# Sums of adj's quarters issued singly and after the first batch's split, with the planner's ranks set anew

## The chip, the core and the metric

The kernel runs on one core of a Trainium2 chip. The metric is the device time of one execution in microseconds (us). Five engines work side by side, each through its own instructions in a fixed order: TensorE (PE, matrix products and transposes), VectorE (DVE), ScalarE (ACT), GpSimd (POOL) and SyncE (SP, which here issues nearly all DMAs). They wait for each other by semaphores.

## The reference, cut to what matters

`x` is 16 batches of 1024 nodes with 128 features, `adj` one symmetric 1024 x 1024 matrix of zeros and ones. A graph attention layer comes first, then five steps of a gated recurrent unit over the graph, and each of the two is followed by a residual sum and a layernorm:

```python
h = x @ others_weight
e = leaky_relu(u1[:, idx1] + u2[:, idx2])           # u1 = h @ a1, u2 = h @ a2
att = softmax(where(adj > 0, e, NEG_BIG), axis=1)
x = layernorm(x + einsum('bik,bkl->bil', att, h) + x @ self_weight)

def step(h, _):
    m_in = einsum('nm,bmd->bnd', adj, h)             # m_out is the same product
    av = concatenate([m_in, m_out], axis=-1)
    u3 = h @ u3_w.T + u3_b
    z = sigmoid(av @ w3_w.T + w3_b + u3)
    r = sigmoid(av @ w4_w.T + w4_b + u3)
    hv = tanh(av @ w5_w.T + w5_b + (r * h @ u5_w.T + u5_b))
    h = (1.0 - z) * h + z * hv
# five steps, then
x = layernorm(x + h)
```

The product that costs most is `adj @ h`, done once for each batch and step.

## The kernel before, in words

**A planner sets the order.** The program doesn't emit its instructions where it describes them. Each piece of work is handed to `Plan.add` (L55) with its engine, an assumed length, a rank (smaller is more urgent), the function that emits it, and what it reads and writes. `Plan.order` (L74) then goes through a list schedule: whenever an engine is free in its assumed time, it takes the ready piece with the smallest rank. Only the resulting order is kept. It is emitted, and on the chip every engine works through it strictly as it stands, each piece held up by semaphores until what it reads is there. The assumed lengths and lags decide nothing else. The ranks come from `rank_of(b, s)` for a batch's step (ten more for each pair of batches, 4.2 more for each step), from `rank0(b)` for a batch's attention layer, and from a table of small offsets `D`: `m` for the copies of an adj product out of PSUM, `pu`, `pr`, `pz`, `pv` for the products of the gates, `u`, `r`, `z`, `hv` for their ScalarE work and `h` for VectorE's update of the state, `tr` and `o` for the way out of a step and of the kernel, `l1` to `l8` for the stages of the attention layer. `l3` is the stage in which the scaled features are split (below).

**Layer 0** (`layer0(b)`) computes, for each batch, the features `hx` with one 131-wide product per 128 nodes (L652), the exponentials of the logits, their sums over the neighbours (L807, DVE, with `adj` as a mask), and scales `rz` (L826 to L834). For batch 0 `rz` comes in two halves of four columns. Then each 128-row piece of `hx` is scaled and split into two fp32r numbers, a rounded upper half on ACT (L856) and the remainder, the lower half, on DVE (L862). Both halves for both of the two scalings lie in four `blk` tiles of four pieces. PE multiplies them by `adj` (`ps_acc_po`, L615), adds the residual (L919, L933), turns the result back (L565), and a layernorm follows (L521 and L523 on DVE, L527 to L534 on POOL, L542 on ACT). `own_weights` (L467) prepares the weights and biases of layer 1. `ahead` (L444) computes the residual products of batches 4 to 7 early (`ps_ahead`, L455) from loads of `x` into the tiles `r_x` and `z_x`; the planner gives these products to PE where nothing more urgent is ready.

**Layer 1** works on pairs of batches. For six of the forty pair-steps (`PLAIN`) `messages` uses plain products with the four quarters Y11, Y12, Y21, Y22 of `adj`: eight accumulating products for each half of a batch (`ps_acc`, L615). For the others it uses a scheme of seven products instead of eight, in which sums of quarters of `adj` (T1 to T4, the tile `tab`, 4 x 4 pieces of 128 x 512) are multiplied by sums of the pair's states (`s1` to `s4`). Its seven products share the banks a, b and c (`ps_acc_a`, `gz`, `ps_acc_c`), and in bank a the results are copied out while the accumulation goes on (L1130 to L1164). `gates` then computes for each half of a batch the gates r and z and the candidate hv: u (L1186) into a bank, copied to `gz` on ACT (L1189), products with `m` (L1196), tanh (L1199), r*h on DVE (L1206), products L1212 and L1213, tanh (L1221), and three DVE operations that update `hT` (L1224, L1227, L1230). `leave` turns `hT` and sends it through DRAM to the next step (T, X, G), or through PE (L565), split again by L603 and L607. Sixteen `look_at` pieces load halves of `adj` once more, one at a time through one buffer (`look`), and count zeros and ones on DVE (L1386, L1372).

**The lines that the change touches.** `sums_of_adj(c)` (L499) makes the four table pieces for row group c. Before, it is two pieces of planned work of two DVE operations each, which always stand together:

```python
dve(2 * V, 1 + c / 4, t13, reads=y, writes=[(("tab",), c, 0)])
dve(2 * V, 1 + c / 4, t24, reads=[*y, (("tab",), c, 0)], writes=[(("tab",), c, 1)])
```

Their rank is 1 to 1.75, larger than that of batch 0's attention (`first` is -62), so that the planner puts them where DVE would otherwise be idle; they can start once the four quarters are in SBUF.

Of the kernel before, what the change touches and what calls it, by code (L numbers as in the profile page):

```python
# [19 lines left out]
NC = N // P  # L20
# [117 lines left out]
def kernel(  # L138
# [79 lines left out]
    def exact(pools):  # L218

        def pool(name, bufs, space=None):  # L220
# [5 lines left out]
        tab = table.tile([P, 4, NC // 2, HALF], F32R, tag="tab", name="tab")  # L226
# [28 lines left out]
            "rstd": (3, [P, 2, 4], F32, None),  # L255
            "D": (6, [P, HALF], F32, bass.MemoryType.DRAM),
            "X": (24, [P, HALF + 16], F32, bass.MemoryType.DRAM),
# [30 lines left out]
        R, F, TR, V, A = 233, 858, 109, 605, 640  # L288
# [4 lines left out]
        def dve(*a, **k):  # L293
            plan.add("DVE", *a, **k)
# [5 lines left out]
            plan.add("SP", *a, **k)  # L300


        D = dict(m=-0.4, pu=1.4, u=1.2, pr=0.8, pz=1.4, r=1.7, pv=1.0, z=1.3, hv=-0.6, h=1.6, tr=1.6, o=5.8, ln=2.9)
        D.update(out=4.4, l1=-9, l2=-4, l3=-3, l4=-4, l5=-7, l6=-1.5, l7=-1, l8=-2)

        def on_pe(b, what):

# [6 lines left out]
        def rank_of(b, s):  # L314
            return 10 * (b // 2) + 4.2 * s + (LATER if b == B - 1 and plain(b // 2, s) else 0)

        def rank0(b):
            return 10 * (b // 2) - 1 * (1 - b % 2) + -1.0 - 6 * (b // 2 == 1)
# [21 lines left out]
        def early_loads():  # L340
# [28 lines left out]
            writes=[(boot, "early"), (ws, "early"), (x0, "early"), (("xt", 1), "early"), *((t, "early") for k in staged for t in k)],  # L369
# [97 lines left out]
        def own_weights():  # L467
            pb_ = ("ps", "g", "b")
            pe(150, -4.6, lambda: column_(pb_, slice(2 * P, 3 * P), 5), reads=[(ws, "b"), (("rz", 0), 1)], writes=[(pb_, 0)])
            dve(160, -4.3, lambda: nc.vector.tensor_copy(bias, T(pb_)[:, 0:5]), reads=[(pb_, 0)], writes=[(("bias",), 0)])  # L470
            dve(1000, -4.2, sums, reads=[(boot, "late"), (("bias",), 0), (("uw",), 0), (("rz", 0), 1)], writes=[(("wm",), 0)])

        def adj_tables(c):
            st = staged[c // 2]

            def left(copy):
                copy(adj[:, c, 0:HALF], T(st[0])[:, c % 2])

            def right():
                nc.scalar.activation(adj[:, c, HALF:N], T(st[1])[:, c % 2], AF.Identity, accum_out=cnt[:, c : c + 1])  # L480

            if c < 4:
                dve(420, -60, lambda: left(nc.vector.tensor_copy), reads=[(st[0], 0)], writes=[(("A",), c, 0)])
            else:
                act(A, -60, lambda: left(nc.scalar.copy), reads=[(st[0], 0)], writes=[(("A",), c, 0)])
            act(640, -50, right, reads=[(st[1], 0)], writes=[(("A",), c, 1)])
# [12 lines left out]
        def sums_of_adj(c):  # L499
            def f(x):  # L500
                return x(c).bitcast(F32)

            def t13():
                nc.vector.tensor_tensor(T1(c), f(Y11), f(Y12), ALU.subtract)
                nc.vector.tensor_tensor(T3(c), f(Y22), f(Y12), ALU.subtract)

            def t24():
                nc.vector.scalar_tensor_tensor(T2(c), f(T1), -1.0, f(Y22), ALU.mult, ALU.subtract)
                nc.vector.scalar_tensor_tensor(T4(c), f(T2), -1.0, f(Y21), ALU.mult, ALU.subtract)

            y = [(("A",), c + 4 * i, j) for i in range(2) for j in range(2)]
            dve(2 * V, 1 + c / 4, t13, reads=y, writes=[(("tab",), c, 0)])
            dve(2 * V, 1 + c / 4, t24, reads=[*y, (("tab",), c, 0)], writes=[(("tab",), c, 1)])


        def layernorm(key, g, rank, after, src, dst, write, sg=1, short=False):
# [108 lines left out]
        def layer0(b):  # L625

            first = rank0(b) - (60 if b == 0 else 0)
            rank = first + D["l1"]
            xt, hx, pb, u, us, uu, ud = (
# [147 lines left out]

            rank = first + D["l2"]

# [19 lines left out]

            rank = rank0(b) + D["l2"]  # L800
            junk = ("junk", b)
# [42 lines left out]
            if b == 0:  # L844
                own_weights()
            rank = rank0(b) + D["l3"]
            size = 1 if b == 0 else 4
# [196 lines left out]
        def messages(q, s, k):  # L1044
# [8 lines left out]
            def from_dram(b, g, i):  # L1053
                t, x = ("G", b, s, g), ("X", b, s, g)
                turn = [(("turn",), k, i - 1) if i else (("turn",), k - 1, 3)]
                entered = [(("hT", x), "in") for x in (one, two)] if s == 0 else []
                sp(0, rank, lambda: T(t), reads=[(x, 0), *turn, *entered], writes=[(t, "place"), (("turn",), k, i)], lag=0)
                back(x, t, rank, [(t, "place")])
                return t
# [34 lines left out]
            if plain(q, s):  # L1094
                for b in (one, two):
# [5 lines left out]
                    for e in range(2):  # L1101
                        bank, m = ("ps", "acc", b, s, e), ("m", b, s, e)
                        for g in range(2):
# [5 lines left out]
                            reads=[(bank, 0)],  # L1109
                            writes=[(m, 0)],  # L1110
# [1 line left out]
                return [[(("m", b, s, e), 0) for e in range(2)] for b in (one, two)]  # L1112

            blk = {k: ("blk", q, s, k) for k in ("x11", "x12", "x22", "s1", "s2", "s3", "s4")}
            t = [(("tab",), c, k) for c in range(4) for k in range(2)]
            f11, f12, f21, f22 = (from_dram(x, g, 2 * (x == two) + g) for x in (one, two) for g in range(2))
            halves(blk["x11"], f11)
            halves(blk["x12"], f12)
# [10 lines left out]
            a, b, c = (("ps", "acc", q, s, "a"), ("gz", q, s), ("ps", "acc", q, s, "c"))  # L1129
            m = {(x, e): ("m", x, s, e) for x in (one, two) for e in range(2)}  # L1130
# [276 lines left out]
        ahead()  # L1407
        for c in range(NC):
            adj_tables(c)
        for c in range(NC // 2):  # L1410
            sums_of_adj(c)
        for b in range(B):
            layer0(b)
        pairs = [(q, s) for q in range(B // 2) for s in range(STEPS)]
        for k, (q, s) in enumerate(sorted(pairs, key=lambda x: rank_of(2 * x[0], x[1]))):
            soon = messages(q, s, k)
            for b in (2 * q, 2 * q + 1):
                gates(b, s, soon)
                leave(b, s)
        for i in range(2 * NC):  # L1420
# [6 lines left out]
            reads=[  # L1427
                *((("seen",), b, k) for b in range(B) for k in range(2)),
                *((("count",), i) for i in range(2 * NC)),
                (("bad",), 0),  # L1430
                (("bad",), 1),
            ],
            writes=[(("rstd", "ends"), 0)],
# [6 lines left out]
            reads=[(("ps", "t", "flag"), 0)],  # L1440
            writes=[(("flag",), 0)],
# [208 lines left out]
    with ExitStack() as pools:  # L1650
        exact(pools)
# [51 lines left out]
```

## Time and profile before

| what | value |
|---|---|
| time, median of 3 runs | 1466.1 us (1465.45 to 1467.84) |
| the profiled execution, its own time | 1464.59 us |
| its span | 1462.4 us (2.2 us lie around it) |
| granted TensorE clock, mean | 0.996 |
| PE busy | 1440.0 us, 98% of the span, 5026 instructions |
| DVE busy | 1163.3 us, 80%, 2752 instructions |
| ACT busy | 896.7 us, 61%, 1792 instructions |
| POOL busy | 205.2 us, 14%, 323 instructions |
| DMA | 174.20 MB, 119 GB/s over the span |
| one 512-wide table sum (L504, L505, L508, L509) | 0.68 to 0.69 us each, 16 of them, 22.2 to 85.1 us from the start |
| landing of a `look` load, where the profile could match it | 2.6 us |

A busy share is an average over stages. An engine at 98% leaves 2% of time in which it wasn't working, and where that time lies, and what ended each of those waits, is what tells of a change of order. The profile has for that the waits by engine, with what released each; the timeline, with the idle time ahead of an instruction in square brackets; and the windows, which give the busy time of each engine within a stretch of the span.

### The profile page before, as it was taken

To read this page: it belongs to the slowest core of one execution; us is meant where nothing else is said; L and a number is where in the kernel's file an instruction comes from. 1 tells how busy PE (TensorE), PEld (TensorE's weight loads), DVE (VectorE), ACT (ScalarE), POOL (GpSimd) and SP (SyncE) were. 2 spreads that over 40 slices of the span, in tenths; PEclk is the share of its full clock that TensorE was granted. 3 is DMA by queue.
4 is the path that set the end of the run, shared out by engine and by line. 5 is a ranking of instruction groups with operands and counts; after the bars stand their busy time and mean duration, and the time that the engine had idled before them with its cause. 6 is when DMAs were issued, how large, how long until landed. Compare 5 with 4: busy or idle time off the path is not lost.

```text
span 1462.4 us, 17792 instructions
## 1 busy us (share of the span) xinstructions
PE 1440.0 (98%) x5026; PEld 901.1 (62%) x5026; DVE 1163.3 (80%) x2752; ACT 896.7 (61%) x1792; POOL 205.2 (14%) x323
## 2 busy tenths in 40 slices
PE   8999999999999999999999999999999999999996
PEld 7666666656566666665666556666666665656663
DVE  6895788978888888888988788886999877766434
ACT  5566564666656665766655776566666656554543
POOL 0321000113110130110301121101201103000201
PEclk9999999999999999999999999999999999999998
DMA  7425234555344553454434543455433544223201
GB/s 251 137 73 180 73 87 134 148 163 154 84 137 127 158 135 97 137 145 138 109 108 130 162 134 88 118 148 167 125 86 93 159 140 109 70 70 87 72 0 31
DMA packets 188033, 174.20 MB, mean 119 GB/s; under 512 B 34240, under 2 KB 137367, under 8 KB 187927
## 3 DMA queue, kind: packets, MB, share of 16 engines
q1 hardware_dynamic: 182562, 156.41, 38.3%
q0 software_dynamic: 4800, 15.73, 3.3%
q8 instruction: 41, 0.67, 0.2%
q10 hardware_dynamic: 564, 0.85, 0.2%
q14 instruction: 66, 0.53, 0.1%
HBM read 95.68 MB, written 77.24 MB: 118 GB/s over the span
## 4 chain that ended last, share of the span: by engine, by line
PE 88%; DMA 4%; DVE 3%; ACT 1%; issue 1%; SPq 1%; POOL 1%; POOLq 0%; DVEq 0%; ACTq 0%
PE ps_acc_a L615 17%; PE ps_g_r L1186 9%; PE ps_g_r L1196 9%; PE ps_g_v L1213 8%; PE gz L1196 8%; PE ps_g_v L1212 8%; PE ps_acc_c L615 8%; PE ps_acc_po L615 8%; PE ps_acc L615 5%; PE gz L615 4%; PE ps_g_ph L652 2%; DMA G<-X 1%; PE ps_acc_px L919 1%; PE ps_acc_po L933 1%; SPq L583 1%
## 5 line engine op out<-in xcount | busy, mean ns | idle before, releaser
L1213 PE MATMUL ps_g_v<-r,u5h 128*128 128x512 f32 x320 | 163.6, 593 | 1.5 <-DVE r L1206 1.5
L1212 PE MATMUL ps_g_v<-m,wm 128*128 128x512 f32 x320 | 163.4, 592 | 0.0
L1196 PE MATMUL gz<-m,wm 128*128 128x512 f32 x320 | 159.6, 592 | 0.0
L1196 PE MATMUL ps_g_r<-m,wm 128*128 128x512 f32 x320 | 158.5, 592 | 0.7 <-ACT gz L1189 0.6
L1224 DVE TENSOR_TENSOR hv<-hv,hT 128x512 f32<-128x512 f32 x160 | 109.4, 685 | 55.9 <-ACT hv L1221 55.2
L1186 PE MATMUL ps_g_r<-hT,u 128*128 128x512 f32 x320 | 153.4, 592 | 0.0
L615 PE MATMUL ps_acc_a<-tab,blk_s 128*128 128x512 f32 x544 | 147.8, 413 | 1.5 <-ACT m L1135 1.4
L1199 ACT ACTIVATE r<-ps_g_r,bh 128x512 f32<-128x512 f32 x160 | 109.2, 687 | 62.9 <-PE ps_g_r L1196 62.9
L1206 DVE SCALAR_TENSOR_TENSOR r<-r,hT 128x512 f32<-128x512 f32 x160 | 108.8, 684 | 43.4 <-ACT r L1199 42.9
L615 PE MATMUL ps_acc_po<-adj,blk 128*128 128x512 f32 x512 | 135.6, 413 | 0.0
L1199 ACT ACTIVATE z<-gz,bh 128x512 f32<-128x512 f32 x160 | 109.4, 686 | 23.9 <-PE gz L1196 23.4
L615 PEld LDWEIGHTS ps_acc_a<-tab,blk_s 128*128 128x128 f32 x544 | 101.2, 188 | 35.9 <-issue 9.1
L615 PEld LDWEIGHTS ps_acc_po<-adj,blk 128*128 128x128 f32 x512 | 95.8, 188 | 32.0 <-issue 8.4
L1189 ACT COPY gz<-ps_g_r 128x512 f32<-128x512 f32 x160 | 91.3, 572 | 37.0 <-PE ps_g_r L1186 35.3
L1230 DVE SCALAR_TENSOR_TENSOR hT<-hv,hT 128x512 f32<-128x512 f32 x160 | 108.1, 678 | 2.3
L1227 DVE SCALAR_TENSOR_TENSOR hv<-z,hv 128x512 f32<-128x512 f32 x160 | 108.0, 677 | 1.9 <-ACT z L1199 0.9
L1213 PEld LDWEIGHTS ps_g_v<-r,u5h 128*128 128x128 f32 x320 | 60.5, 189 | 78.8 <-issue 61.3
L1196 PEld LDWEIGHTS gz<-m,wm 128*128 128x128 f32 x320 | 60.7, 190 | 76.6 <-issue 76.6
L527 POOL TENSOR_SCALAR rstd_y<-mv_y 128x4 f32<-128x4 f32 x32 | 16.7, 522 | 649.2 <-DVE mv_y L523 647.8
L615 PE MATMUL ps_acc<-adj,blk_h 128*128 128x512 f32 x384 | 103.4, 417 | 0.6 <-ACT blk_h L603 0.3
L603 ACT CAST blk_s<-G 128x512 fp32r<-128x512 f32 x136 | 82.2, 618 | 34.0 <-DVE G L1077 28.1
L573 DVE STREAM_TRANSPOSE T<-hT 128x512 f32<-128x512 f32 x138 | 96.4, 701 | 2.3 <-DMA X<-T 2.0
(196 smaller groups left out, 2584.9 us busy)
## 6 DMA issues: line engine op xcount, KB each, us to landing
G<-X SPq DMA_DIRECT2D x140, 256.0 KB, 2.8
X<-T SPq DMA_DIRECT2D x552, 64.0 KB, 1.8
yd<-y POOLq DMA_DIRECT2D x32, 256.0 KB, 3.1
D_y<-T_y SPq DMA_DIRECT2D x112, 64.0 KB, 1.9
F_y<-D_y SPq DMA_DIRECT2D x28, 256.0 KB, 2.6
X<-y SPq DMA_DIRECT2D x28, 256.0 KB, 2.0
D_b<-T_b SPq DMA_DIRECT2D x112, 64.0 KB, 2.2
F_b<-D_b SPq DMA_DIRECT2D x28, 256.0 KB, 3.0
```

Source lines behind the costliest of these rows:

```text
L573: nc.vector.transpose(T(t).rearrange("p (b c i) -> p b c i", b=4, c=4), turned(src()))
L615: nc.tensor.matmul(T(bank), T(blk)[:, k, c, :], right(c), start=(first and i == 0), stop=(last and i == len(terms) - 1), skip_group_check= ...
L1186: nc.tensor.matmul(T(pr), u3, h(), start=True, stop=True)
L1189: nc.scalar.copy(T(pz), T(pr))
L1196: nc.tensor.matmul(T(p_), wm[:, j, :], T(m), start=False, stop=True, skip_group_check=True)
L1199: nc.scalar.activation(T(t), T(p_), AF.Tanh, bias=bh[:, j : j + 1], scale=0.5 * sg)
L1206: lambda r=r, h=h: nc.vector.scalar_tensor_tensor(T(r), T(r), 1.0, h(), ALU.add, ALU.mult),
L1212: nc.tensor.matmul(T(pv), wm[:, 2, :], T(m), start=True, stop=False)
L1213: nc.tensor.matmul(T(pv), u5h, T(r), start=False, stop=True)
L1224: nc.vector.tensor_tensor(T(hv)[:, w], T(hv)[:, w], h()[:, w], ALU.subtract)
L1227: nc.vector.scalar_tensor_tensor(T(hv)[:, w], T(z)[:, w], 1.0, T(hv)[:, w], ALU.add, ALU.mult)
L1230: nc.vector.scalar_tensor_tensor(h()[:, w], T(hv)[:, w], 0.5, h()[:, w], ALU.mult, ALU.add)
```

## The change

Four things are changed, all of them in what the planner is told. No instruction is added or removed: the counts on each engine are the same, and so are the shapes.

- In `sums_of_adj` the two double pieces become four single ones of half the length, in the order T1, T3, T2, T4, with T2 depending on T1 and T4 on T2. Their rank stays.
- Each of them now also reads the last lower half of batch 0's second scaling, so that the planner puts none of them ahead of that split. `sums_of_adj` is called after `layer0(0)` for this.
- `messages` waits for all sixteen pieces of the table by their new names.
- Seven offsets in `D` move: `m` from -0.4 to -0.8, `u` from 1.2 to 0.8, `pz` from 1.4 to 1.2, `hv` from -0.6 to -0.4, `h` from 1.6 to 1.2, `o` from 5.8 to 6.6, and `l3` from -3 to -2.

```diff
-        D = dict(m=-0.4, pu=1.4, u=1.2, pr=0.8, pz=1.4, r=1.7, pv=1.0, z=1.3, hv=-0.6, h=1.6, tr=1.6, o=5.8, ln=2.9)
-        D.update(out=4.4, l1=-9, l2=-4, l3=-3, l4=-4, l5=-7, l6=-1.5, l7=-1, l8=-2)
+        D = dict(m=-0.8, pu=1.4, u=0.8, pr=0.8, pz=1.2, r=1.7, pv=1.0, z=1.3, hv=-0.4, h=1.2, tr=1.6, o=6.6, ln=2.9)
+        D.update(out=4.4, l1=-9, l2=-4, l3=-2, l4=-4, l5=-7, l6=-1.5, l7=-1, l8=-2)
...
-            def t13():
+            def t1():
                 nc.vector.tensor_tensor(T1(c), f(Y11), f(Y12), ALU.subtract)
+
+            def t3():
                 nc.vector.tensor_tensor(T3(c), f(Y22), f(Y12), ALU.subtract)
 
-            def t24():
+            def t2():
                 nc.vector.scalar_tensor_tensor(T2(c), f(T1), -1.0, f(Y22), ALU.mult, ALU.subtract)
+
+            def t4():
                 nc.vector.scalar_tensor_tensor(T4(c), f(T2), -1.0, f(Y21), ALU.mult, ALU.subtract)
 
             y = [(("A",), c + 4 * i, j) for i in range(2) for j in range(2)]
-            dve(2 * V, 1 + c / 4, t13, reads=y, writes=[(("tab",), c, 0)])
-            dve(2 * V, 1 + c / 4, t24, reads=[*y, (("tab",), c, 0)], writes=[(("tab",), c, 1)])
+            y.append((("blk", 0, 1, 1), NC - 1, 1))
+            for n, (sum_, first) in enumerate(((t1, None), (t3, None), (t2, 0), (t4, 2))):
+                more = [] if first is None else [(("tab",), c, first)]
+                dve(V, 1 + c / 4, sum_, reads=[*y, *more], writes=[(("tab",), c, n)])
...
-            t = [(("tab",), c, k) for c in range(4) for k in range(2)]
+            t = [(("tab",), c, k) for c in range(4) for k in range(4)]
...
         for c in range(NC):
             adj_tables(c)
-        for c in range(NC // 2):
-            sums_of_adj(c)
         for b in range(B):
             layer0(b)
+            if b == 0:
+                for c in range(NC // 2):
+                    sums_of_adj(c)
```

## The prediction

> **What bounds the kernel now.** The busy shares came first: PE 98%, DVE 80%, ACT 61%. PE sets the time, but 2% of it is idle, and the change touches only the order of work, so the question is where those 2% lie. The windows answer it. Columns: stretch in us from the start, its length, PE busy with instructions, then PE's weight loads, DVE, ACT, POOL, granted clock, DMA share, GB/s.
>
> ```profile
> 28.00:80.00 52.00, 50.31 (x234) 35.73 (x235) 44.48 (x162) 32.44 (x88) 14.74 (x20) 1.00 0.41 133
> 80.00:160.00 80.00, 78.52 (x295) 50.41 (x294) 61.37 (x163) 48.38 (x105) 10.34 (x20) 1.00 0.40 119
> 160.00:400.00 240.00, 237.55 (x802) 146.77 (x802) 199.35 (x466) 147.04 (x295) 29.42 (x40) 1.00 0.45 124
> 400.00:1370.00 970.00, 969.98 (x3252) 599.54 (x3251) 801.14 (x1814) 613.96 (x1195) 141.59 (x217) 1.00 0.44 121
> 1447.00:1462.40 15.40, 2.94 (x13) 2.20 (x12) 7.51 (x27) 3.07 (x8) 2.96 (x6) 0.60 0.20 57
> ```
>
> From 400 to 1370 us PE is busy 969.98 of 970 us: nothing can be won there by any order, only lost. Idle are 1.7 us of 28 to 80, 1.5 of 80 to 160, 2.5 of 160 to 400, the first 28 us, and 12.5 of the last 15.4. The waits of PE (total us, times, longest) name them:
>
> ```profile
> PE ps_ahead L455 <- DMA r_x<-in_x_dram: 2.5, 1, 2.5
> PE ps_g_v L1213 <- DVE r L1206: 1.5, 2, 1.0
> PE ps_acc_a L615 <- ACT m L1135: 1.4, 1, 1.4
> PE ps_t_b L565 <- ACT y L542: 1.0, 1, 1.0
> PE ps_acc L615 <- ACT blk_h L603: 0.3, 1, 0.3
> PE ps_acc_a L615 <- ACT m L1137: 0.3, 1, 0.3
> PE ps_acc L615 <- DVE blk_h L607: 0.2, 1, 0.2
> ```
>
> The timeline of PE shows where in the head they stand. Columns: start, us, instruction, in brackets the idle time before it and what ended it.
>
> ```profile
> 27.86 1.10 PE L455 MATMUL ps_ahead<-r_x,wsi 128*128 128x512 f32 x2 [2.47 <-DMA r_x<-in_x_dram]
> ...
> 50.62 1.38 PE L565 MATMUL ps_t_b<-ident,y 128*128 128x128 f32 x4 [1.04 <-ACT y L542]
> 52.32 0.50 PE L615 MATMUL ps_acc<-adj,blk_h 128*128 128x512 f32 x1 [0.32 <-ACT blk_h L603]
> ```
>
> A busy PE hides small stalls, since the modelled ends of matmuls overlap their successors. From start to start, against the unhindered spacing (0.233 us an fp32r product of 512, 0.858 a pair of fp32 ones), I count 3.2 to 3.4 us lost between 28 and 80 us, 1.1 and 0.7 at the two L1213 waits at 142.09 and 148.02, about 3.3 between 160 and 372, and 0.54 in two spots of the saturated part (715 and 1062 us).
>
> [...] the table sums measure 681 (L504) and 678 (L505). A double piece was two instructions already, so singles cost nothing more. [...]
>
> **The change part by part.** Work is the same on every engine; only positions move. The positions below are those the planner's rules give for the changed table of ranks, counted in groups of like products ("row").
>
> *Sums, single and after the split.* Before, L504 and L505 stand at 22.20 and 22.80 us, ahead of the chain for u and `rz` (23.40 to 25.1) and the lower halves (25.11 on). Each costs 0.60 us of DVE issue, so the chain comes 2 x 0.60 = 1.2 us earlier after. That is worth nothing by itself: PE's next row is `ps_ahead`, held until 27.86 by a load issued at 22.14 that lands 5.6 us later, in both kernels. The two double pieces that stood at 48.18 and 64.79 us move as well. The sums now come one at a time, the last at about 117 us by my count. Their first reader is the c product of the first seven-product pair-step (190.5 us in the trace before; about 150 us in the new order), so 30 us of cover remain and their lateness costs 0.
>
> *The head, 28 to 80 us.* The ranks (l3 by one, m, h) change what PE finds here. Before, six `ps_ahead` stand together at 43.83 to 48.57, then PE meets batch 0's turned-back output (50.62) and its split (52.32, 53.05) with nothing to do. After, all eight `ps_ahead` stand early (rows 23 to 37), and three groups of batch 1's attention products (rows 45, 46, 50; 8 x 0.233 = 1.9 us each) come before batch 0's first message product (row 60 instead of 49). The chain to cover runs from the layernorm's statistics at 46.52 through POOL (about 2 us), L542 (1.51), L565, L603 (0.62) and L607 (0.69). I laid these durations with 0.2 us a hop along the new order and find PE fed from 27.86 to about 78 us. The 3.2 to 3.4 us go; I take -3.0 (bounds -1.0, if half the new cover is late, and -3.4).
>
> *80 to 160 us.* The stalls at 142.09 and 148.02 (1.8 us) are VectorE's r*h behind look counts:
>
> ```profile
> 133.79 0.43 DVE L1386 TENSOR_SCALAR junk_look<-look 128x512 f32<-128x512 f32 x1 [4.58 <-DMA look<-in_adj_dram]
> ...
> 140.27 0.43 DVE L1386 TENSOR_SCALAR junk_look<-look 128x512 f32<-128x512 f32 x1 [5.32 <-DMA look<-in_adj_dram]
> ...
> 141.35 0.69 DVE L1206 SCALAR_TENSOR_TENSOR r<-r,hT 128x512 f32<-128x512 f32 x1
> ```
>
> There is one look buffer, so a look is issued when the one before is counted; here it took from 134.95 to 140.27, 5.3 us. The new order has the same pattern: two looks stand ahead of the third and fourth r*h of the first step (DVE rows 239, 245 before 244, 248; needed at PE rows 142 and 144, near 149 and 150.5 us). With the page's 2.6 us of landing nothing stalls; with 5.3 us up to 3.5 us do. Bounds: -1.8 and +3.5; I take -1.8 + 0.4 for one late transpose at about 115 us, so -1.4.
>
> *160 to 400 us.* The largest spot is 1.56 us at 371.40, where a bank a copy waited for ACT behind a layernorm's scaling held 4.88 us by POOL. The new ranks shuffle this, and I see no pattern. Unchanged at 3.3, bounds 0 and 8: 0 (-3.3 to +4.7).
>
> *The saturated part.* In bank a PE goes on accumulating only when ACT has copied the last product out; the copy's turnaround is the cover plus the stall seen, 0.97 + 0.27 = 1.24 us. Two such gaps have a cover of 0.97 before. After, three have 0.86 and one 0.91: 3 x 0.38 + 0.33 = 1.5 us against 0.54: +1.0 (bounds 0 and +2). The lead of `m` by 0.4 gives more cover at the median (2.16 against 1.75 us), and the long loop through DRAM keeps its least cover (18.8 against 17.5 us), so I expect nothing else.
>
> *The tail.* PE's order over the last 130 us is the same; 0.
>
> Sum: -3.0 - 1.4 + 0 + 1.0 = -3.4 us. Against the profiled execution: span 1462.4 - 3.4 = 1459.0, its time 1464.59 - 3.4 = 1461.2. The median shown is 1.5 us above the profiled time, so 1466.1 - 3.4 = 1462.7; I write 1462.5.
>
> **The rivals.**
> A: the stalls only move. Each loss in the head is one late chain on a PE with nothing else ready, and new rows meet new chains. For it: PE had six spare `ps_ahead` as filler at 44 to 49 us and the new order has used them up by row 37. Against it: batch 1's products replace them. The gain left is the -1.0 of the head with +1.0 of the banks: 1466.
> B: slower, through VectorE behind the looks. Place: DVE rows 239 to 249. Price: with landings of 5.3 us for both, 3.5 us at row 144 instead of nothing, twice if the next two looks do the same, less the 1.8 saved, on a head that gives -1.0, with the banks' +1.0: 2 x 3.5 - 1.8 = 5.2, so 1471. It decides once a look takes over about 3.5 us while G loads run. For it: 4.58 and 5.32 us of waiting above. Against it: 2.49 us for the look at 144.53.
> C: the sums do nothing and only the ranks matter; the time is the forecast's, and an order with the old sums would show it.
> D: every stall between 28 and 400 us goes, and the banks lose nothing: 3.3 + 1.8 + 3.3 = 8.4 us, 1457.7. That is the floor, since the rest is saturated or the tail.
>
> **How the numbers follow.** Chances: the forecast with C 0.42, A 0.24, B 0.26, D 0.08. What a measurement here can tell from no change is 0.2%, 2.9 us: 1463.2 to 1469.0. The forecast's own range is 1460 to 1464.5, so a little of it falls within; a little of A lies on the faster side. Faster 0.50, same 0.24, slower 0.26. Range: from D's floor of 1457.5 to B's 1471.
>
> **What would show it.** Right: PE in 28 to 80 us busy without a wait over 0.3 us; no L1213 wait on L1206 near 150 us; table sums ending near 117 us with no reader waiting; 400 to 1370 us still filled but for some 1.5 us at bank a copies. Wrong: a new PE wait on L1206, on `blk` or on G before 400 us, or a saturated part no longer full. A change of DMA timing in the head, above all of the load that holds PE until 27.86, would move everything after it.

## The result, and the profile after

The changed kernel takes 1461.0 us (median of 20 runs, 1457.48 to 1466.42), the kernel before 1466.09 us in 20 runs beside it (1462.33 to 1468.69). The ratio is 0.9968, 95% interval 0.9958 to 0.9979. The profiled execution of the changed kernel has a time of 1462.54 us and a span of 1460.8 us.

The same windows as before (columns as in the prediction), of the kernel after:

```profile
28.00:80.00 52.00, 51.77 (x243) 39.38 (x244) 44.15 (x159) 31.73 (x86) 13.36 (x20) 0.97 0.40 134
80.00:160.00 80.00, 78.76 (x292) 49.97 (x291) 64.20 (x174) 50.05 (x113) 10.84 (x20) 1.00 0.44 129
160.00:400.00 240.00, 239.01 (x809) 148.41 (x808) 200.86 (x459) 145.04 (x282) 25.18 (x40) 1.00 0.43 123
400.00:1368.00 968.00, 966.81 (x3239) 597.43 (x3237) 794.36 (x1810) 615.23 (x1205) 138.22 (x217) 1.00 0.43 121
```

The head from 28 to 80 us is full but for 0.23 us, which lie before its first instruction at 28.23. But the granted clock there is 0.97, and the stretch from 400 us on, which was full, now lacks 1.2 us. The waits of PE in the kernel after:

```profile
PE ps_ahead L455 <- DMA r_x<-in_x_dram: 2.3, 1, 2.3
...
PE ps_g_r L1202 <- ACT gz L1195: 1.4, 2, 0.8
...
PE ps_acc_a L621 <- ACT m L1141: 1.2, 1, 1.2
PE ps_acc_a L621 <- ACT m L1143: 0.5, 1, 0.5
```

The waits on r*h (L1206 before, L1212 now) and on batch 0's turned-back output are gone. What is left between the load at 28 us and the tail hangs nearly all on ACT: its copies `gz` and `m`.

Both kernels were profiled a second time. The table gives PE's loss by stretch, counted as in the prediction from start to start against the unhindered spacing, at the same amount of PE work in each kernel (the times are rough):

| stretch, us | before | again | after | again | change | predicted |
|---|---|---|---|---|---|---|
| 0 to 28 | 7.60 | 7.23 | 7.92 | 7.34 | +0.3, +0.1 | 0 |
| 28 to 33 | 1.24 | 1.24 | 2.50 | 0.94 | +1.3, -0.3 | 0 |
| 33 to 80 | 3.42 | 3.41 | 0.00 | 0.03 | -3.4, -3.4 | -3.0 |
| 80 to 172 | 2.06 | 2.24 | 2.34 | 2.90 | +0.3, +0.7 | -1.4 |
| 172 to 404 | 3.59 | 4.23 | 1.65 | 1.95 | -1.9, -2.3 | 0 |
| 404 to 1320 | 0.22 | 0.23 | 1.71 | 3.38 | +1.5, +3.2 | +1.0 |
| 1320 to the last wait | 2.54 | 2.33 | 2.43 | 2.27 | -0.1, -0.1 | 0 |
| sum | 20.65 | 20.92 | 18.55 | 18.81 | -2.1, -2.1 | -3.4 |

So the sum came to -2.1 us where -3.4 were foretold, and that partly by luck: 80 to 172 us went the wrong way, and 172 to 404 us, put at 0, made up for it. What the experiments had to settle: whether the sums or the ranks fill the head; what the new losses of 80 to 172 and of 404 on are; and what happens at 28 to 33 us.

### The profile page after: what moved, and what is told of

It reads as the page before. It is cut to its first block, busy times and chain, and to the rows that moved or that the text cites. A ratio compares the mean times of both kernels' runs of the same rounds, so it can differ in the third digit from the quotient of the medians.

```text
span 1460.8 us, 17800 instructions
## 1 busy us (share of the span) xinstructions
PE 1439.6 (99%) x5026; PEld 903.2 (62%) x5026; DVE 1159.4 (79%) x2752; ACT 897.0 (61%) x1792; POOL 196.6 (13%) x323
## 4 chain that ended last, share of the span: by engine, by line
PE 88%; DMA 4%; DVE 3%; SPq 1%; ACT 1%; issue 1%; POOL 1%; DVEq 0%; POOLq 0%; ACTq 0%
PE ps_acc_a L621 16%; PE ps_g_r L1202 9%; PE ps_g_v L1218 9%; PE ps_g_v L1219 9%; PE gz L1202 9%; PE ps_g_r L1192 8%; PE ps_acc_c L621 8%; PE ps_acc_po L621 8%; PE ps_acc L621 5%; PE gz L621 4%; PE ps_g_ph L658 1%; SPq L589 1%; PE ps_acc_px L925 1%; PE ps_acc_po L939 1%; DMA look<-in_adj_dram 1%
## 5 line engine op out<-in xcount | busy, mean ns | idle before, releaser
L1212 DVE SCALAR_TENSOR_TENSOR r<-r,hT 128x512 f32<-128x512 f32 x160 | 109.2, 685 | 50.8 <-ACT r L1205 50.6
L621 PE MATMUL ps_acc_po<-adj,blk 128*128 128x512 f32 x512 | 141.5, 423 | 0.0
L533 POOL TENSOR_SCALAR rstd_y<-mv_y 128x4 f32<-128x4 f32 x32 | 13.5, 422 | 683.8 <-DVE mv_y L529 659.2
L613 DVE TENSOR_TENSOR blk_s<-G,blk_s 128x512 fp32r<-128x512 f32 x136 | 92.0, 681 | 8.6 <-ACT blk_s L609 8.1
```

The source lines that it names most:

```text
L613: lambda: nc.vector.tensor_tensor(half(1), src(), half(0), ALU.subtract),
L621: nc.tensor.matmul(T(bank), T(blk)[:, k, c, :], right(c), start=(first and i == 0), stop=(last and i == len(terms) - 1), skip_group_check= ...
L1212: lambda r=r, h=h: nc.vector.scalar_tensor_tensor(T(r), T(r), 1.0, h(), ALU.add, ALU.mult),
```

## The experiments

Four groups of kernels ran, each group on one chip, with its own runs of the kernel before. Losses are counted as in the table above (in `fill`, the transposes that it adds count as lost time).

**The two halves alone: `ranks` and `sums`.** `ranks` is the kernel before with the seven new offsets, `sums` the kernel after with the old ones:

```diff
-        D = dict(m=-0.4, pu=1.4, u=1.2, pr=0.8, pz=1.4, r=1.7, pv=1.0, z=1.3, hv=-0.6, h=1.6, tr=1.6, o=5.8, ln=2.9)
-        D.update(out=4.4, l1=-9, l2=-4, l3=-3, l4=-4, l5=-7, l6=-1.5, l7=-1, l8=-2)
+        D = dict(m=-0.8, pu=1.4, u=0.8, pr=0.8, pz=1.2, r=1.7, pv=1.0, z=1.3, hv=-0.4, h=1.2, tr=1.6, o=6.6, ln=2.9)
+        D.update(out=4.4, l1=-9, l2=-4, l3=-2, l4=-4, l5=-7, l6=-1.5, l7=-1, l8=-2)
```

> The kernel before with the seven new ranks alone; the sums stay double and ahead of the split. If the ranks carry the change, the stalls of 28 to 80 us (3.2 us of start-to-start loss in the kernel before) are gone: in this order eight ps_ahead and three groups of batch 1's attention products stand ahead of batch 0's turned-back output, and the ratio is 0.996 to 0.998. If the sums' place is what counts, some 3 us of loss stay there and the ratio is 0.999 to 1.002.

> The changed kernel with the seven old ranks: the sums alone. If moving the sums does nothing but fill idle VectorE time, the ratio is 0.999 to 1.001 and the waits at ps_t_b and ps_acc near 50 us (1.0, 0.3, 0.2 us) stay. If moving them re-plans what stands behind them, those waits go: in this order 8.0 us of products stand between the turned ps_t_y of batch 0 and its ps_t_b, against 5.7 before, for a chain of some 7 us. Then the ratio is 0.997 to 0.999.

The kernels after and before went along once more, unchanged:

> The changed kernel once more, for a second trace. If the half clock granted at about 30 to 33 us in the first trace follows from the 2.3 us of idle PE and the phase of whatever samples it, it need not be there again, and then ps_p (16 transposes) takes about 2.0 us instead of 3.66 and the span is some 1.3 us shorter than 1460.8. If it belongs to the new order, it is there again.

> The kernel before once more, for a second trace. The same question from the other side: its PE is idle 2.5 us at the same place. If the half clock is a matter of phase, it can turn up here too; if it belongs to the new order, the clock stays at 1.00 between 28 and 36 us. The loss of 3.2 us between 44 and 53 us must be there again, as must the look landings of about 5 us, if these are properties of the order and not of one execution.

| kernel | median us (runs) | ratio to before [95%] | lost 28-33 | 33-80 | 80-172 | 172-404 | 404-1320 | in all |
|---|---|---|---|---|---|---|---|---|
| ranks | 1463.09 (14) | 0.9988 [0.9980, 0.9996] | 2.79 | 1.75 | 1.90 | 1.32 | 2.74 | 21.07 |
| sums | 1462.64 (13) | 0.9992 [0.9980, 1.0003] | 0.95 | 1.71 | 1.88 | 1.89 | 1.47 | 18.31 |
| after again | 1461.94 (14) | 0.9984 [0.9970, 0.9999] | 0.94 | 0.03 | 2.90 | 1.95 | 3.38 | 18.81 |
| before again | 1465.16 (13) | 1.0010 [1.0001, 1.0018] | 1.24 | 3.41 | 2.24 | 4.23 | 0.23 | 20.92 |

By time the four can hardly be told apart: the kernel before differs from itself by 0.1%. By the traces they can. Neither half fills the head: of the 3.4 us between 33 and 80 each leaves 1.7. So "only the ranks matter" is wrong as it stood: with the old sums, the planner sets PE's order differently from the same ranks. Which part of the new sums does that, the single pieces or their later place, no run separates. In `ranks` more of the `ps_ahead` stand ahead of batch 0's products, and PE meets a transpose that waits for DVE's `rz`. (The 2.79 us at 28 to 33 in `ranks` hold a stretch of half clock, of which below.) Timeline of PE, kernel `ranks`:

```profile
45.98 0.63 PE L565 MATMUL ps_t_y<-ident,yT 128*128 128x128 f32 x4 [1.58 <-DVE rz L826]
```

In the kernel after, products of `ps_acc_po` stand at 44.60 and no such wait appears.

**Are the sums' places worth anything on the chip? `sums_back`.** The order of the kernel after, with the four sums of row group 0 put back early in DVE's order (two ahead of the second half of `rz`, two ahead of the lower halves); PE's order doesn't change:

```diff
...
-            for i in plan.order():
+            order = [i for i in plan.order() if i not in mark["sums"]]
+            for i, op in zip((mark["rz"], mark["lo"]), (mark["sums"][:2], mark["sums"][2:])):
+                order[order.index(i) : order.index(i)] = op
+            for i in order:
```

> The changed kernel with the four sums of row group 0 alone put back where the kernel before had them, T1 and T3 ahead of the second half of rz, T2 and T4 ahead of the six lower halves; PE's order is untouched. If the sums' place costs nothing on the chip itself, as the prediction has it, since ps_ahead holds PE until r_x lands, no wait is added in 28 to 80 us over 0.3 us. If the split is held up, ps_acc_po waits for blk for 1.2 us (two sums) or up to 2.4 us (four) near 33 us, and the ratio is 0.001 to 0.0017 above the changed kernel's.

Measured: 1462.06 us (11 runs), ratio 0.9973 [0.9964, 0.9983]; nothing lost between 33 and 80 us. Windows of `sums_back`:

```profile
28.00:80.00 52.00, 52.00 (x249) 38.67 (x249) 45.86 (x166) 34.71 (x96) 12.66 (x20) 1.00 0.38 124
```

Put early, these four sums delay nothing: their place in DVE's order is worth 0, as predicted (the other twelve were not moved). What the sums bring, they bring through the plan.

**Which rank? `l3_old`.** The kernel after with `l3` at -3 as before.

```diff
-        D.update(out=4.4, l1=-9, l2=-4, l3=-2, l4=-4, l5=-7, l6=-1.5, l7=-1, l8=-2)
+        D.update(out=4.4, l1=-9, l2=-4, l3=-3, l4=-4, l5=-7, l6=-1.5, l7=-1, l8=-2)
```

> The changed kernel with one rank put back, l3 = -3. Its order of the head is that of the kernel with the sums alone (ps_t_b after five ps_ahead, batch 0's message products right behind it), so that if l3 alone shapes the head, waits at ps_acc <- blk_h of 0.6 us and some 1.5 us of loss from 45 to 75 us come back, and the other six ranks, which set what follows, keep their part: ratio 0.998 to 0.9995. If the head is shaped by the sums alone and l3 does nothing, the head loses nothing and the ratio is that of the changed kernel.

Measured: 1461.75 us (13 runs), ratio 0.9979 [0.9968, 0.9991]; 1.83 us lost between 33 and 80, close to the 1.71 of `sums`. So the head is filled by two edits together: the sums take one half of the 3.4 us, and with them in place the step of `l3` takes the other. The six other ranks leave the head as it is. By its time `l3_old` can't be told from the kernel after.

**The load that PE waits for at 26 us, and the clock behind it: `later`, `fill`, `later_b`.** The clock of 0.97 from 28 to 80 lies in one place. Windows of the kernel after, where PE stood idle from 25.98 to 28.23:

```profile
28.00:30.00 2.00, 1.77 (x12) 1.03 (x13) 0.24 (x2) 0.64 (x2) 0.00 (x0) 0.90 1.03 389
30.00:32.00 2.00, 2.00 (x11) 2.00 (x11) 1.93 (x9) 0.82 (x3) 0.00 (x0) 0.50 0.87 289
32.00:34.00 2.00, 2.00 (x11) 1.86 (x11) 0.14 (x2) 1.00 (x4) 0.00 (x0) 0.75 0.06 23
```

The shortfalls add up to half clock for 3.4 us ((0.10 + 0.50 + 0.25) x 2 / 0.5). PE's timeline there, the kernel after and then the same kernel's second trace:

```profile
29.60 3.66 PE L756 MATMUL ps_p<-ident,u 128*128 128x128 f32 x16
```

```profile
27.65 1.10 PE L455 MATMUL ps_ahead<-r_x,wsi 128*128 128x512 f32 x2 [2.08 <-DMA r_x<-in_x_dram]
...
29.02 2.05 PE L756 MATMUL ps_p<-ident,u 128*128 128x128 f32 x16
```

The same sixteen transposes took 3.66 us in one execution and 2.05 in the other, which is the +1.3 us of the table. The traces of `ranks`, `l3_old` and `unblock` have such a stretch at the same place (0.97 from 28 to 80 us in each, with 0.50 to 0.62 from 30 to 32). `later` moves batch 1's `ps_pairs` and `ps_p`, which need no load, ahead of the first `ps_ahead` in PE's order; `later_b` makes the same move in the kernel before; `fill` instead adds 20 transposes of the identity into that product's bank, which it then overwrites:

```diff
...
+            order = plan.order()
+            front = [i for i in order if i in mark["front"]] + [mark["px"]]
+            order = [i for i in order if i not in front]
+            at = 1 + max(order.index(d) for i in front for d in plan.ops[i][4] if d not in front)
+            order[at:at] = front
...
```

```diff
-                    def px_(bank=bank, x=x):
+                    def px_(bank=bank, x=x, first=(b, e) == (AHEAD[0], 0)):
+                        for j in range(20 if first else 0):
+                            nc.tensor.transpose(T(bank)[:, 0:P], ident, ident)
```

> The changed kernel with one move on PE: batch 1's ps_pairs and its two ps_p groups (1.9 us of products) stand ahead of the first ps_ahead instead of behind it; every other engine's order is as in the changed kernel. If PE's 2.3 us of idle ahead of that ps_ahead are only the wrong order (the load is late, ps_pairs is ready by 25 us), ps_pairs starts near 26 us instead of 29.2, the wait on r_x falls below 0.6 us, no half clock follows it, and the end comes 2 to 3.5 us earlier than the changed kernel's: ratio 0.994 to 0.997. If the po products behind are then held by the lower halves on DVE, the 1.9 us come back as a wait at ps_acc_po and the ratio is that of the changed kernel, 0.997 to 0.9985.

> The changed kernel with 20 more transposes of the identity (2.2 us) in the bank of the first ps_ahead, ahead of its product, which overwrites them: PE works through the wait for r_x. If the half clock seen at 28 to 33 us in two traces out of five comes of that idle stretch, it is 1.00 there in this trace and the runs with a mean clock of 0.994 or 0.995 become rare; the median falls by 0.5 to 1.3 us against the changed kernel: ratio 0.996 to 0.998. If the half clock has another cause, the share of such runs stays (about 6 of 20) and nothing is won.

> The kernel before the change with the same one move on PE (ps_pairs and ps_p of batch 1 ahead of the first ps_ahead). If PE's idle ahead of ps_ahead is a matter of that order alone, it goes here too, while the 3 us of waits at 50 to 53 us stay: 1.5 to 2.5 us less than before, ratio 0.998 to 0.999. If those chains start earlier too, their waits at 50 us can only stay or grow, up to all that was won: 1.000.

| kernel | median us (runs) | ratio to before [95%] | lost 0-28 | 28-33 | 33-80 | 404-1320 | in all |
|---|---|---|---|---|---|---|---|
| later | 1460.30 (6) | 0.9964 [0.9949, 0.9978] | 5.62 | 0.63 | 0.03 | 5.15 | 17.03 |
| fill | 1464.93 (13) | 1.0000 [0.9991, 1.0009] | 7.56 | 0.38 | 0.60 | 6.11 | 20.3 |
| later_b | 1463.92 (14) | 0.9998 [0.9990, 1.0006] | 6.09 | 0.76 | 5.69 | 0.22 | 21.71 |

`later` wins what the wait took and shows no half clock (1.00 from 28 to 80 us). But from 404 us on it loses 5.2 us, where the kernel after loses 1.7 and 3.4. So the gain over that kernel is 1.5 to 1.8 us of loss and 2.0 of span, no more than the lower edge of what was expected, and by its time `later` can't be told from it. `later_b` wins 1.5 us ahead of 28 us too, and loses it again. The old order's waits at 50 us are there, as long as before (1.04, 0.32 and 0.23 us of idle time); what is new in its 5.7 us is some 1.5 us of half clock right behind them, and 0.4 us at a product that waits for the split at 34 us. Windows of `later_b`:

```profile
50.00:52.00 2.00, 1.40 (x5) 0.58 (x4) 1.48 (x5) 1.97 (x7) 1.64 (x4) 0.93 0.99 340
52.00:54.00 2.00, 2.00 (x5) 1.61 (x6) 1.93 (x8) 2.00 (x8) 0.00 (x0) 0.50 0.40 157
```

`fill` keeps the clock at 1.00 from 28 to 80 us in its trace, and is no faster than the kernel before. What was to show that the half clock comes of that wait didn't come: 5 of its 13 runs still have a mean clock of 0.995, about the share of the kernel after (6 of 20). Its trace loses 6.1 us after 404 us, most of it at the kinds of wait described next (2.4 us at 525, 0.6 at 541, 1.0 at 1180, 1.5 at 1201 us). Why the median is as long as that, also in the runs with 0.996 and 0.997, the one trace can't tell. That stays open.

**What the new losses are.** A single wait is counted here as the prediction counted the 1.56 us at 371.40 us: from start to start, less the unhindered spacing of the product ahead (0.43 us for an fp32 one). First 404 us on. ACT works in its own order, and one of its pieces waits for something slow with `m` or `gz` copies behind it. In the kernel after, ACT and then PE near 1199 us:

```profile
1193.53 0.59 ACT L1141 COPY m<-gz 128x512 f32<-128x512 f32 x1 [1.17 <-PE gz L621]
1198.10 0.62 ACT L1037 COPY hT<-F_b 128x512 f32<-128x512 f32 x1 [3.98 <-DMA F_b<-D_b]
1198.62 0.58 ACT L1141 COPY m<-ps_acc_a 128x512 f32<-128x512 f32 x1
```

```profile
1199.26 2.12 PE L621 MATMUL ps_acc_a<-tab,blk_s 128*128 128x512 f32 x8 [1.17 <-ACT m L1141]
```

ACT waited 3.98 us for a state of batch 15 that comes back through DRAM, the bank a copy stood behind it, and PE behind that. The second kind, in the second trace of the kernel after, ACT and then POOL:

```profile
522.32 1.65 ACT L548 ACTIVATE o<-o,rstd_o 128x128 f32<-128x128 f32 x4 [2.92 <-POOL rstd_o L543]
...
524.58 0.57 ACT L1195 COPY gz<-ps_g_r 128x512 f32<-128x512 f32 x1
```

```profile
515.70 4.18 POOL L533 TENSOR_SCALAR rstd_o<-mv_o 128x4 f32<-128x4 f32 x1 [1.85 <-DVE mv_o L529]
```

A layernorm's scaling waited for POOL, where one operation on 128x4 numbers took 4.18 us. In the first trace the same operation at the same place took 0.57 us, and there is no loss:

```profile
517.71 0.57 POOL L533 TENSOR_SCALAR rstd_o<-mv_o 128x4 f32<-128x4 f32 x1 [1.85 <-DVE mv_o L529]
```

The stall at 371.40 us in the kernel before was of the same kind. POOL, ACT and PE there:

```profile
363.21 3.77 POOL L527 TENSOR_SCALAR rstd_o<-mv_o 128x4 f32<-128x4 f32 x1 [2.25 <-DVE mv_o L523]
```

```profile
369.23 1.65 ACT L542 ACTIVATE o<-o,rstd_o 128x128 f32<-128x128 f32 x4 [4.88 <-POOL rstd_o L534]
370.78 0.56 ACT L1135 COPY m<-ps_acc_a 128x512 f32<-128x512 f32 x1
```

```profile
371.40 1.90 PE L615 MATMUL ps_acc_a<-tab,blk_s 128*128 128x512 f32 x7 [1.40 <-ACT m L1135]
```

`unblock` takes four such pieces back by two or three places in ACT's order, behind the copies that need not wait (three scalings with the DMA that sends their result, and batch 15's state); `both` adds the move of `later` to that:

```diff
+SPOTS = ((("scale", "o", 0, 0), 2), (("scale", "o", 2, 1), 3), (("scale", "o", 3, 1), 2), (("in", 15, 0), 2))
...
+            for what, n in SPOTS:
+                i = mark[what]
+                at = order.index(i)
+                acts = [k for k in order[at + 1 :] if plan.ops[k][0] == "ACT"]
+                moved = [i] + ([mark["sent", what[2], what[3]]] if what[0] == "scale" else [])
+                order = [k for k in order if k not in moved]
+                at = order.index(acts[n - 1]) + 1
+                order[at:at] = moved
```

> The changed kernel with four ACT instructions moved two or three places back on ACT alone: the scalings of the output layernorm of (batch 0, half 0), (2, 1) and (3, 1), and the copy of batch 15's first half from F_b. In the traces of the changed order each of them waits 1.6 to 4.5 us for POOL or a DMA with a copy for PE behind it. If that is what PE loses between 330 and 1250 us (3.4 to 6 us in the last traces of this order), the waits at about 338, 525, 541 and 1199 us fall below 0.4 us each, the loss from 390 to 1300 us of work falls below 1 us, and the ratio is 0.995 to 0.997. If the cover of bank a's copies is at fault, as the prediction has it, the stalls stay at 0.4 to 1 us each whatever stands ahead on ACT, and the ratio is that of the changed kernel, 0.997 to 0.9985.

> The move on PE (batch 1's ps_pairs and ps_p ahead of the first ps_ahead) and the four moves on ACT together. The two act in different stretches and should add: 1.9 us at 26 to 28 us, no half clock, and 2 to 4 us between 330 and 1250 us: span 1454 to 1456.5 us, ratio 0.993 to 0.9955. If what is won early only meets a longer wait later (the DMAs' pace), the span stays at 1458 or above.

| kernel | median us (runs) | ratio to before [95%] | lost 80-172 | 172-404 | 404-1150 | 1150-1320 | in all |
|---|---|---|---|---|---|---|---|
| unblock | 1460.11 (8) | 0.9971 [0.9959, 0.9983] | 2.33 | 0.25 | 0.72 | 1.94 | 18.14 |
| both | 1457.86 (6) | 0.9961 [0.9949, 0.9973] | 3.17 | 0.91 | 0.57 | 1.93 | 14.04 |

The scaling near 338 us was what stood in the way there: in the kernel after PE lost 0.6 and 1.2 us behind it (two traces), in `unblock` nothing. ACT in the kernel after, then the windows of `unblock`:

```profile
336.24 1.65 ACT L548 ACTIVATE o<-o,rstd_o 128x128 f32<-128x128 f32 x4 [1.58 <-POOL rstd_o L543]
...
338.36 0.57 ACT L1143 ACTIVATE m<-ps_acc_a 128x512 f32<-128x512 f32 x1
```

```profile
160.00:400.00 240.00, 240.00 (x814) 149.24 (x813) 202.13 (x464) 146.21 (x286) 25.19 (x40) 1.00 0.44 124
```

(`both` loses 0.91 again in this stretch, most of it before an `m` copy at 334 us, and another wait, at 322 us, comes and goes from trace to trace.) Near 525 us the loss is gone, but so is its cause: POOL's operation there took 0.57 us in the trace of `unblock` and wasn't slow in `both` or `both2` either. It took 4.18 us in four of the five traces with the old place of the scalings (the second of the kernel after, `sums_back`, `later`, `fill`). Whether the moves, which shift POOL's own sends too, took the slow operation away, no run shows. At 539 us the third scaling waited 1.58 us for POOL, and PE lost nothing by it.

By its time `unblock` can't be told from the kernel after, and 404 to 1320 us it still loses 2.7 us, where less than 1 was expected.

The state of batch 15 was not cured. The wait at 1199 went, and the next one, for the second half of the same batch, held PE instead, 4 us on. PE in `unblock`:

```profile
1203.43 2.13 PE L625 MATMUL ps_acc_a<-tab,blk_x 128*128 128x512 f32 x8 [1.58 <-ACT m L1148]
```

Then 80 to 172 us. DVE, ACT and PE in the kernel after:

```profile
136.35 0.43 DVE L1392 TENSOR_SCALAR junk_look<-look 128x512 f32<-128x512 f32 x1 [3.01 <-DMA look<-in_adj_dram]
...
138.63 2.15 DVE L1083 TENSOR_TENSOR G<-G,G 128x512 f32<-128x512 f32 x3
```

```profile
139.35 0.62 ACT L609 CAST blk_s<-G 128x512 fp32r<-128x512 f32 x1 [2.76 <-DVE G L1083]
139.88 0.58 ACT L1114 COPY m<-ps_acc 128x512 f32<-128x512 f32 x1
140.36 1.07 ACT L1195 COPY gz<-ps_g_r 128x512 f32<-128x512 f32 x2
```

```profile
141.00 1.98 PE L1202 MATMUL ps_g_r<-m,wm 128*128 128x512 f32 x4 [0.83 <-ACT gz L1195]
```

Read downwards: DVE stood 3.01 us behind a look's load, so the sums of G came late, so ACT waited 2.76 us to split one of them, so the `gz` copy behind the split came late, and PE lost 1.0 us (1.6 in the second trace). `both2` is `both` with that look moved behind the lower half and the sums of G on DVE, and the second half of batch 15 one place back on ACT (the loads next in SP's order move along):

```diff
...
+            k = mark["look", 1]
+            sums = [i for i in order[order.index(k + 1) + 1 :] if plan.ops[i][0] == "DVE"][:4]
+            moved = [k, k + 1, mark["look", 2] - 1]
+            order = [i for i in order if i not in moved]
+            at = order.index(sums[-1]) + 1
+            order[at:at] = moved
```

> The kernel of both, with two more moves: the copy of the last input slice of batch 15 on ScalarE one place back (and the load behind it on SP), and the two operations of look 1 on VectorE behind the split's lower half and the three g sums near 133 us (and the next look's load on SP). TensorE and POOL keep their order. Theory that VectorE standing behind the look's load is what delays the splits and the gz copies on ScalarE, and so TensorE near 136-141 us (2.2 us lost in both, 1.4 to 2.0 in the kernel after): that loss falls to 0.4-1.0 us, the loss at 1199 us (1.9 us in both) below 0.5, the span comes to 1452.5-1454.5 and the ratio to 0.993-0.996. Rival, the waits only move on to the next operation in ScalarE's order: losses of the same size a few us later, span at 1455.5 or above, ratio 0.996 or more.

Measured: 1458.72 us (6 runs), ratio 0.9956 [0.9939, 0.9973], span 1458.9. The wait at 136 to 141 us is gone (1.8 us in `both`), and the loss at 1199 fell from 1.5 in `both` to 0.2: the causes named were the causes. But PE now waits elsewhere. PE in `both2`, then DVE:

```profile
151.65 1.13 PE L1230 MATMUL ps_g_v<-r,u5h 128*128 128x512 f32 x2 [1.52 <-DVE r L1223]
...
1207.32 1.13 PE L1230 MATMUL ps_g_v<-r,u5h 128*128 128x512 f32 x2 [1.29 <-DVE r L1223]
```

```profile
149.23 0.43 DVE L1406 TENSOR_SCALAR junk_look<-look 128x512 f32<-128x512 f32 x1 [2.62 <-DMA look<-in_adj_dram]
...
150.91 0.68 DVE L1223 SCALAR_TENSOR_TENSOR r<-r,hT 128x512 f32<-128x512 f32 x1
```

An r*h behind a later look, as in the kernel before. From 80 to 172 us `both2` loses 3.30 us, `both` 3.17; the rival on record, that the waits only move on, holds for this step. The ratio fits both theories; the span and the losses speak for the rival. (Of the 2.8 us between the two spans, 2.0 lie before 28 us, where the two don't differ.)

## Why the prediction was right, and where it was not

**The head, -3.0: right.** It measured -3.4 in both pairs of traces, and the waits at 50.62, 52.32 and 53.05 us went. (The 0.2 us a hop was an allowance: in that chain in the trace of before, from L523 to POOL and from L603 and L607 to what waited for them, 0.03 to 0.08 us lie between the recorded end and the next start.) The reason given held only by half: it put the fill down to the ranks, and `ranks`, `sums` and `l3_old` show that it takes the new sums as well.

**The place of the sums, 0: right.** They end at 119 us instead of the 117 counted, with their first reader at 157 us, and `sums_back` shows no cost of putting them early. Issued singly, the sixteen took 0.68 to 0.70 us each, against 0.67 to 0.69 in double pieces. Rival C, that they do nothing at all, was too strong: through the planner they change PE's order, as `ranks` beside the kernel after shows.

**80 to 160 us, -1.8 + 0.4 = -1.4: wrong.** The two L1206 waits went, as the -1.8 says, and a small loss near the foretold place came (0.5 us at 117 us, on a copy of ACT). The step that failed is that this alone would take their place: PE lost another 1.0 to 1.6 us on a `gz` copy. The look was named as the danger (rival B), but the prediction followed it only to r*h on DVE and PE. It didn't follow it through the sums of G to ACT, whose order has the `gz` copy behind the split. The price of B, 5.2 us net of the saving, was also too high: one look did harm, not two with 3.5 us each.

**160 to 400 us, 0: wrong, by -1.9 and -2.3.** "I see no pattern" was the step. The 371.40 us stall went (1.56, and 1.64 in the second trace of before), as did one at 242 us (0.45 and 0.95); a new one came at 338 us (0.6 and 1.2). The largest of both orders are of one kind: a layernorm's scaling on ACT, waiting for POOL, with a copy for PE behind it. That could have been looked for in the new order, since it shows in the positions alone. The bounds (-3.3 to +4.7) did hold it.

**The saturated part, +1.0: right sign, wrong mechanism.** It measured +1.5 and +3.2. The prediction took it from the short covers of bank a (0.86 and 0.91 us against a turnaround of 1.24). That turnaround was read off stalls that cost nothing: at 715 and 1062 us in the kernel before, PE's next start came 0.298 us after the last instead of 0.028, but the one after that came 0.362 us later instead of 0.631, so that the two together took the unhindered 0.66 us. The losses that could be seen are instead ACT waiting for a DMA at 1199 us (1.33 and 0.75) and for POOL at 525 and 541 us (2.0, in one of the two traces); no stall of 0.3 to 0.4 us at bank a's copies appears.

**The first 28 us and the clock: not in the sum.** The prediction warned of that load only as of a change in DMA timing. The load came as before (5.7 us from its issue to PE's start, 22.14 to 27.86 us in the kernel before and 22.57 to 28.23 after); what was missed is the half clock that followed PE's idle time there in the profiled execution (0.50 for 3.41 us), worth 1.3 us, and didn't in the second trace (1.00 from 28 to 80 us).

**The sum and the median.** The traces give -2.1 us of loss and -1.6 and -1.8 of span, the medians -5.1; in the repeat on one chip -3.2, or -2.5 against the 43 runs of the kernel before in that group. The gain of the median is thus known only as some 2.5 to 5 us. The forecast, 3.6 down to 1462.5, lies within, and how near it came is luck. One profiled execution isn't the median: over the 43 runs of the kernel before in the first group and the first 20 of the kernel after, those with the same mean granted clock differ by 3.4 us at 0.995 (1465.9 to 1462.5), 3.2 at 0.996 (1463.5 to 1460.3) and 3.6 at 0.997 (1463.0 to 1459.4). Within the first group, against the 14 repeats of the kernel after, it is 2.1 at 0.996 and 2.7 at 0.997, nearer to the traces. But 20 of the 43 had 0.995 or less, and 6 of the 20 (3 of the 14 repeats). The mean tells of the half clock: the five traces with such a stretch ahead of the tail have 0.995, the nine without it 0.996 or 0.997. That half clock follows the old order's stalls at 50 to 53 us in some executions, as it did in the trace of `later_b` (0.50 from 52 to 54 us), would explain the rest; this is an estimate, since both traces of the kernel before itself have 1.00 there.

## What to carry to other kernels

When a queue worked in order holds one piece that waits for something slow (a load, a slow small operation on another engine), list what stands behind it on that engine and who waits for that, and follow it over two engines, not one. A stall taken out of a nearly full engine is worth what the next late chain leaves of it: `later` lost 1.8 to 3.4 us of its gain at the head again behind 404 us, and in `both2` the waits that were taken away came back at r*h. And a late start alone is no stall: look whether the next start is late by as much, as it wasn't at 715 and 1062 us. Where differences are 0.2%, compare losses stretch by stretch in traces taken twice, since identical kernels differed by 0.1% in time. The best version found is `both`, 1457.86 us at 0.9961 [0.9949, 0.9973]; its interval overlaps that of the kernel after, and what speaks for it beyond the median is the loss of 14.0 us in its trace against 18.6 and 18.8. Of that lead 1 to 2 us are the luck of its first loads: with the same order of PE there, `later` lost 1.1 us more ahead of 28 us, and `both2` 2.0.

## What the runs showed of the hardware

- After 2.25 us without PE work (25.98 to 28.23 us in the kernel after) the clock was half for 3.41 us, from 29.59 to 33.00; after 2.08 us in another execution of the same kernel it stayed full. In `later_b`, with half clock from 51.73 to 55.14 us, gaps of 1.04 and 0.32 us, with work between them, went ahead of it, and one of 0.23 lies across its start.
- Why the same wait was followed by it in one execution and not in the next can only be estimated, from the fourteen traces. Ahead of the tail, each stretch that a trace records at one clock is a multiple of 3.41 us long: 23.89 us at full clock, 3.41 at half and 1416.53 at full in the kernel after; 1443.84 at full in its second trace; 44.37, 3.41 and 1396.05 in `later_b`. Counted in steps of 3.41 us from where a trace's record of the clock begins, the borders fell differently on the work in each execution: one lies at 26.18 us in the kernel after, one at 26.67 in the kernel before. The time that PE loses in one step, from start to start, is 2.27 to 2.74 us in the five steps ahead of a half clock (2.44 in the step from 26.18 us in the kernel after, 2.74 in that from 48.32 us in `later_b`), and at most 2.12 us in all the others up to 1400 us. In the second trace of the kernel after a border of the steps divides the wait, and the larger part is 1.85 us. The kernel before has two places where a step can lose more than 2.27 us (up to 2.71 us near 27 and 2.75 near 51 us), the kernel after only the first (2.52); in `fill`, the wait at 525 us can come to 2.38, so that its runs at 0.995 may have the half clock there, which is not shown. All this was read from the traces afterwards; no run was made to test it.
- POOL's first operation of a layernorm (L533, 128x4 numbers) took 0.22 to 0.66 us in 63 of 64 executions in the first trace of the kernel after, and 2.99 in the one at 532.00 us (2.98 or 2.99 near there in `unblock`, `both`, `both2` and `later` too). In the second trace the one at 515.70 us took 4.18 (and so at that place in three other kernels); ACT's wait of 2.92 us behind it shows the delay from another engine. What held it is open.
